# A four-layer graph network on one core: the engines' order from a planner with due times, or written out step by step

## The chip, the core and the metric

The kernel runs on one core of a Trainium2 chip. A core has five engines that run their own instruction lists and wait for each other through semaphores: TensorE (PE, matrix products into the banks of PSUM), VectorE (DVE), ScalarE (ACT), GpSimd (POOL) and SyncE (SP). Transfers are issued by SP or by POOL and carried by 16 transfer engines. The metric is the time of one execution on the device, in microseconds (us); lower is better.

## The reference

The input x holds 32 graphs of 512 nodes with 256 features, in float32, and one 512 x 512 adjacency matrix serves all graphs. Four layers follow each other; each ends with `x = layernorm(x + layer(x))`.

- Layer 0: attention with 8 heads of 32 features and the adjacency as mask, then a layernorm, a two-step perceptron (256 to 256, relu, 256 to 256) and another layernorm.
- Layer 1: graph attention with one head. The score of a pair of nodes is `leaky_relu(s1[n] + s2[m])`, masked, softmax, times the projected features.
- Layer 2: attention with full scores `h1 h2^T`, leaky relu, mask, softmax, times `h3`, relu.
- Layer 3: as layer 1 with 4 heads of 64 features, and elu at the end.

Node numbers matter nowhere but in the adjacency: if x, the adjacency's rows and columns and the output are all numbered in another order, the same thing is computed.

## The kernel before, in words

A graph's 512 nodes lie in 4 chunks of 128 partitions. The kernel does not loop over graphs at run time: Python writes out all steps of all 32 graphs and sorts them.

**Steps.** `fast_path` describes each graph as some 300 steps. A step names its engine, an assumed duration, what it reads and what it writes (`Plan.__call__`, through the helpers `dve`, `act`, `pool`). The work areas are slots of a few kinds: 8 PSUM banks, 8 "p" buffers (128 x 2048 numbers, for unnormalised attention weights), 9 "t", 7 "y", 6 "x" and so on.

**Layer 0** (`layer0`): x is transposed on PE (`transposed`, L932), q, k and v are projected (`project_t`, `project`, all through `product`, L749). For each half of the heads and each chunk m, `exps` makes the scores of four heads with four 32-row products side by side (L1064), ACT takes their exponential into p (L1068), DVE multiplies p by the adjacency (L1116), and four 32-column products side by side give the weighted sum (L1123). The row sums of the softmax are not taken on PE for each p: POOL issues transfers that add one p to another (`add_dma`, L1002), and only the total goes through PE (`sums`, L1095). In the last graph the sums are taken on PE at once. Then come `heads_out` (L1047), the normalisation (`normalise`) and the perceptron.

**Layers 1 and 3** turn a score into a product of exponentials. `gates` takes an exponential, transposes it on PE (L1212), writes it to DRAM through SP (L1216) and reads it back broadcast to all partitions (L1222). DVE then makes p (L1241 or L1320) and multiplies it by the adjacency (L1244 or L1327), and PE takes the product with the values (L749 in layer 1, L1335 in layer 3). **Layer 2** makes scores on PE, four steps on ACT and DVE, and a product with the values (L749).

**Shapes of TensorE.** Three shapes occur: the full array (128*128, way 0), four row tiles (32*128, way 1, `exps`) and four column tiles (128*32, way 2, L1123, L1335 and the sums). The products of `product` can run in way 0 or in way 2. `Plan.emit` chooses among them along the finished order.

**Order.** Up to six graphs are under way at a time. `Plan.place` simulates the engines with the assumed durations. At each point it takes, among the steps that can start first, the one that is due first. The due time of a step comes from `PACE` (81.87 us per graph), `TENTHS`, `FIRST` and `LAST`, tables that stretch a graph's own course. `START` holds back the first graphs. `safe` refuses a step that could leave too few buffers. The result is one fixed list per engine, and that is what runs on the chip.

**Set-up.** `prepare` loads weights and adjacency through SP, turns the adjacency into a transposed mask with 16 PE transposes (L818), and folds some weights together. These steps go ahead of all others on their engines.

Of the kernel before, what the change touches and what calls it, by code (L numbers as in the profile page):

```python
# [17 lines left out]
P = 128  # L18
# [11 lines left out]
WAYS = 6  # L30
PACE = 81.87
STAY = 0.00
START = (0, 10.17, 59.24, 97.18, 85.64)
EARLY = 186.52

TENTHS = (0, 35.72, 65.32, 68.92, 152.58, 202.32, 246.27, 266.73, 356.34, 362.66, 490.49)
FIRST = (
    (0, 35.72, 65.32, 62.35, 138.44, 202.98, 246.27, 266.73, 356.34, 362.66, 490.49),
    (-28.44, 35.72, 73.98, 55.02, 197, 202.32, 246.27, 266.73, 356.34, 362.66, 490.49),
    (-31.13, 30.72, 65.32, 68.92, 152.58, 202.32, 246.27, 266.73, 356.34, 362.66, 490.49),  # L40
    (0, 35.77, 65.37, 68.97, 152.63, 202.32, 246.27, 266.73, 356.34, 362.66, 490.49),)
LAST = (
    (0, 35.72, 65.32, 68.92, 152.58, 202.32, 246.27, 266.73, 354.73, 363.36, 490.49),
    (0, 35.72, 65.32, 68.92, 152.58, 202.32, 246.27, 266.73, 356.34, 362.66, 490.49),
    (0, 35.72, 65.32, 68.92, 152.58, 202.26, 246.21, 266.73, 356.34, 412.91, 557.81),
    (-0.21, 35.51, 65.11, 68.71, 152.37, 202.11, 226.96, 232.14, 316.44, 341.17, 500.04),
    (-6.23, 29.49, 59.09, 8.93, 61.49, 76.67, 155.18, 191.54, 257.43, 316.36, 394.47),)
# [391 lines left out]
SIGNAL = 70  # L439
SWITCH = 100  # L440
CHANGE = {0: 196, 1: 213, 2: 126}


class Slot:
# [3 lines left out]
    def __init__(self, kind):  # L448
        self.kind, self.index, self.users, self.ends, self.graph = kind, None if kind else 0, 0, 0.0, None
        self.first = self.last = None  # L450


class Op:
    def __init__(self, engine, ns, run, graph, rank, port, lag, tiling, ways):
        self.engine, self.ns, self.run, self.graph, self.rank = engine, ns, run, graph, rank
        self.port, self.lag, self.tiling, self.ways = port, lag, tiling, ways
        self.then, self.missing, self.slots, self.ready = [], 0, [], 0.0


class Plan:  # L460
# [10 lines left out]
    def clear(self):  # L471
        self.ops, self.graph, self.rank, self.start = [], 0, 0, 0.0
        self.log = {}

    def begin(self, graph, start=0.0):


        self.graph, self.rank, self.start = graph, 0, start

    def __call__(self, engine, ns, run, reads=(), writes=(), port=False, lag=0, tiling=0, ways=None):  # L480
        op = Op(engine, ns, run, self.graph, self.rank, port, lag, tiling, ways or {tiling: 0})
        if not op.rank:
            op.ready = self.start
        self.rank += 1
        needs = {}
        for is_write, group in ((False, reads), (True, writes)):
            for item in group:
                slot, part = (item[0], item[1:]) if isinstance(item, tuple) else (item, None)
                if slot not in op.slots:
                    op.slots.append(slot)  # L490
                    slot.users += 1
                    if slot.first is None:
                        slot.first = op.rank
                    slot.last = op.rank
# [19 lines left out]
    def profile(self, graph):  # L514

        ops = [op for op in self.ops if op.graph == graph]
        live = {kind: [0] * len(ops) for kind in self.counts}
        for slot in {id(s): s for op in ops for s in op.slots if s.kind}.values():
            for r in range(slot.first, slot.last + 1):
                live[slot.kind][r] += 1  # L520
        return live

    def place(self, urgency, ways, stay=0.0, early=1e12,):
# [3 lines left out]
        held_by = {g: self.profile(g) for g in {op.graph for op in self.ops}}  # L527
        engines = {e: 0.0 for e in (PE, DVE, ACT, POOL, SP, DMA)}
        waiting = {e: [] for e in engines}
        free = {k: [(0.0, i) for i in range(n)] for k, n in self.counts.items()}  # L530
        todo, held = {}, {}
        for op in self.ops:
            todo.setdefault(op.graph, set()).add(op.rank)
            if not op.missing:
                waiting[op.engine].append(op)
        order, front, ended = sorted(todo), {g: 0 for g in todo}, {}
        port, port_by, end, tiling = 0.0, None, 0.0, 0
        self.trace = []

        def safe(op, kind, new):  # L540
            spare = len(free[kind]) - len(new)
            if spare < 0:
                return False
            have = spare
            for g in order:
                mine = held.get((g, kind), [])
                have += len(mine)
                if g == op.graph:
                    have += len(new)
                    mine = mine + new  # L550
                r, rows = front[g], held_by[g][kind]
                ahead = sorted(s.first for s in mine if s.first > r)
                for i, stop in enumerate(ahead + [len(rows)]):
                    if stop > r and max(rows[r:stop]) + len(ahead) - i > have:
                        return False
                    r = max(r, stop)
                if g == op.graph:
                    return True

        while todo:  # L560
            choice = None
            for e, ops in waiting.items():
                found = []
                for op in ops:
                    if order[0] + ways <= op.graph:
                        continue
                    due = urgency(op)
                    t = max(engines[e], op.ready, ended.get(op.graph - ways, 0.0))
                    if op.graph >= 0:
                        t = max(t, due - early)  # L570
                    if op.port and port_by is not e:
                        t = max(t, port)
                    if choice and t > choice[0]:
                        continue
                    wants = {}
                    for s in op.slots:
                        if s.index is None:
                            wants.setdefault(s.kind, []).append(s)
                    if all(safe(op, kind, new) for kind, new in wants.items()):
                        for kind, new in wants.items():  # L580
                            t = max(t, sorted(free[kind])[len(new) - 1][0])
                        if op.tiling != tiling and e is PE:
                            due += stay
                        found.append((t, due, op))
                if found:
                    best = min(found, key=lambda f: f[:2])
                    if choice is None or best[0] < choice[0]:
                        choice = best
            assert choice, "no instruction can be placed: too few buffers"
            t, _, op = choice  # L590
            if op.engine is PE and op.tiling != tiling:
                t, tiling = max(t, engines[PE] + SWITCH), op.tiling
# [35 lines left out]
    def emit(self, tiling):  # L628
# [16 lines left out]
        for _, op in self.trace:  # L645
            if op.engine is PE:
                tiling[0] = chosen.pop()
            if op.run:
                op.run()
# [817 lines left out]
```

## Time and profile before

| | |
|---|---|
| median of 3 runs | 2868.73 us (2868.06 to 2869.86) |
| the profiled execution | 2871.61 us |
| its span, first to last instruction | 2869.7 us |
| TensorE busy | 2802.0 us (98%) |
| VectorE busy | 2436.6 us (85%) |
| ScalarE busy | 1884.6 us (66%) |
| GpSimd busy | 871.5 us (30%) |
| granted TensorE clock, mean | 0.991 |

The busy time of TensorE counts each matmul from its start to its modelled end, and matmuls overlap. A busy TensorE is therefore not one at its peak: the distance between the starts of two steps tells more than the length of one. Durations below come from the one profiled execution.

### The profile page before, as it was taken

How to read it: one execution, taken by the hardware profiler on the slowest of the kernel's cores; microseconds unless marked ns; L12 is line 12 of the kernel's file. 1: busy time of each engine (PE TensorE's matmuls, PEld its weight loads, DVE VectorE, ACT ScalarE, POOL GpSimd, SP SyncE). 2: the span in 40 equal slices, each digit the busy share in tenths (PEclk: the TensorE clock that was granted, in tenths of full speed). 3: DMA queues.
4: the chain of work that ended last, by engine and by line, in shares of the span. 5: the costliest groups of instructions: out<-in, count | busy, mean ns of one | idle time of the engine just before them, and what ended most of it. 6: DMA issues, size and time to landing. Idle time of an engine off the chain costs nothing.

```text
span 2869.7 us, 49717 instructions
## 1 busy us (share of the span) xinstructions
PE 2802.0 (98%) x19058; PEld 1507.2 (53%) x19058; DVE 2436.6 (85%) x4076; ACT 1884.6 (66%) x4104; POOL 871.5 (30%) x962
## 2 busy tenths in 40 slices
PE   8889999999999999999999999999999999999996
PEld 3345455555555555555555555555555555554562
DVE  5467888988888988888888888998888998889877
ACT  4566667666676666676666676666676766677553
POOL 1223333323333223333323333323333323333312
PEclk9899999999999999999999999999999999999998
DMA  7855777777776777777777777777777777775115
GB/s 168 169 115 122 159 159 151 156 156 149 164 162 151 155 157 149 162 166 149 155 156 149 162 165 154 149 156 148 163 165 157 148 159 149 160 165 114 41 51 139
DMA packets 101188, 425.07 MB, mean 148 GB/s; under 512 B 10256, under 2 KB 46224, under 8 KB 59152
## 3 DMA queue, kind: packets, MB, share of 16 engines
q0 software_dynamic: 49600, 325.08, 57.6%
q1 hardware_dynamic: 51344, 96.75, 11.7%
q8 instruction: 152, 2.49, 0.3%
q14 instruction: 92, 0.75, 0.1%
HBM read 63.38 MB, written 17.10 MB: 28 GB/s over the span
## 4 chain that ended last, share of the span: by engine, by line
PE 87%; DVE 7%; DMA 2%; ACT 2%; issue 2%; POOL 0%; SPq 0%; DVEq 0%; ACTq 0%; POOLq 0%
PE bank L749 54%; PE bank L1064 8%; PE bank L1123 8%; PE bank L1335 7%; PE bank L932 4%; DVE p L1116 3%; PE bank L1047 2%; PE bank L1311 1%; PE bank L1095 1%; PE bank L1015 1%; DVE p L1320 1%; DMA x<-in_x_dram 1%; ACT p L1068 1%; DVE st L973 1%; DMA p<-p 0%
## 5 line engine op out<-in xcount | busy, mean ns | idle before, releaser
L1002 POOL DMA_DIRECT2D p<-p x372 | 323.3, 873 | 1766.4 <-DMA p<-p 587.7
L1116 DVE TENSOR_TENSOR p<-p,edge_t 128x2048 f32<-128x2048 f32 x256 | 628.5, 2464 | 61.4 <-ACT p L1068 61.2
L920 ACT ACTIVATE t<-bank 128x512 f32<-128x512 f32 x640 | 373.1, 595 | 393.6 <-PE bank L1123 129.9
L1068 ACT ACTIVATE p<-bank 128x512 f32<-128x512 f32 x1024 | 537.4, 599 | 81.9 <-PE bank L1064 81.5
L749 PE MATMUL bank<-v,p 128*128 128x257 f32 (+1 forms) x2912 | 468.0, 384 | 4.3 <-DVE p L1244 3.8
L749 PEld LDWEIGHTS bank<-v,p 128*128 128x128 f32 (+1 forms) x2912 | 367.7, 159 | 90.7 <-issue 26.6
L973 DVE BATCH_NORM_STATS2 st<-y 128x6 f32<-128x256 f32 x768 | 316.1, 412 | 36.2 <-POOL y L990 26.6
L1320 DVE TENSOR_SCALAR p<-p,e,e 128x512 f32<-128x512 f32 x512 | 333.1, 684 | 0.4 <-DMA p<-row 0.3
L990 POOL TENSOR_TENSOR y<-y,x 128x512 f32<-128x512 f32 x192 | 275.3, 1441 | 156.7 <-ACT y L1295 98.4
L1327 DVE TENSOR_TENSOR p<-p,edge_t 128x2048 f32<-128x2048 f32 x128 | 310.2, 2423 | 2.2
L1064 PE MATMUL bank<-t,t 32*128 32x512 f32 x2048 | 300.7, 646 | 0.0
L983 ACT ACTIVATE x<-y,rs,rs 128x256 f32<-128x256 f32 x512 | 277.7, 596 | 18.0 <-DVE rs L980 15.1
L1123 PE MATMUL bank<-p,v 128*32 128x512 f32 x2048 | 274.0, 607 | 15.2 <-DVE p L1116 11.4
L1335 PE MATMUL bank<-p,v 128*32 128x512 f32 x2048 | 241.5, 597 | 3.7 <-DVE p L1327 3.2
L749 PE MATMUL bank<-t,wqkv 128*32 128x512 f32 (+1 forms) x944 | 243.8, 596 | 0.9 <-ACT t L920 0.9
L920 ACT ACTIVATE v<-bank 128x264 f32<-128x264 f32 (+2 forms) x384 | 176.1, 459 | 80.0 <-PE bank L749 77.0
L749 PE MATMUL bank<-t,t 128*128 128x512 f32 (+1 forms) x656 | 225.2, 592 | 0.0
L1064 PEld LDWEIGHTS bank<-t,t 32*128 32x128 f32 x2048 | 84.1, 185 | 173.4 <-issue 86.4
L932 PE MATMUL bank<-ident,x 128*128 128x128 f32 x1024 | 149.6, 280 | 14.2 <-DMA x<-in_x_dram 10.3
L974 DVE BATCH_NORM_AGGREGATE mv<-st 128x2 f32<-128x6 f32 x768 | 139.9, 182 | 26.3
L932 PEld LDWEIGHTS bank<-ident,x 128*128 128x128 f32 x1024 | 118.2, 142 | 78.8 <-issue 37.7
L749 PEld LDWEIGHTS bank<-t,t 128*128 128x128 f32 (+1 forms) x656 | 94.3, 167 | 111.2 <-issue 107.2
(119 smaller groups left out, 3855.7 us busy)
## 6 DMA issues: line engine op xcount, KB each, us to landing
p<-p POOLq DMA_DIRECT2D x248, 1024.0 KB, 7.2
p<-p POOLq DMA_DIRECT2D x124, 512.0 KB, 5.8
p<-row SPq DMA_DIRECT2D x32, 1024.0 KB
x<-in_x_dram SPq DMA_DIRECT2D x32, 512.0 KB
out_dram<-x SPq DMA_DIRECT2D x32, 512.0 KB
p<-p SPq DMA_DIRECT2D x31, 512.0 KB
e<-row SPq DMA_DIRECT2D x32, 256.0 KB
t<-in_adj_dram SPq DMA_DIRECT2D x4, 256.0 KB
```

Source lines behind the costliest of these rows:

```text
L749: nc.tensor.matmul(out[c:c + w, :], left[:, c:c + w], right, start=start, stop=stop)
L920: act(170 + n * 0.84, lambda: nc.scalar.activation(to(T(dst)), frm(T(src)), AF.Copy), [src], writes)
L932: nc.tensor.transpose(T(bank)[:, (2 * k + c) * P:(2 * k + c + 1) * P], T(src)[:, c0 + c, k * P:(k + 1) * P], ident)
L973: nc.vector.bn_stats(T(st)[:, c, :], T(y)[:, c, :])
L1002: nc.gpsimd.dma_start(a, b, accum_op=ALU.add)
L1064: nc.tensor.matmul(T(banks[j]), T(kT)[r, g, m * P:(m + 1) * P], T(qT)[r, g, :], start=True, stop=True)
L1068: act(600, lambda j=j: nc.scalar.activation(T(p)[:, j, :], T(banks[j]), AF.Exp, scale=1.0 / math.sqrt(D0)), [banks[j]], [(p, j)])
L1116: dve(2420, lambda p=p, m=m: nc.vector.tensor_tensor(T(p), T(p), T(edge_t)[:, m, :].unsqueeze(1).to_broadcast([P, J, N]), ALU.mult), [p, ( ...
L1123: nc.tensor.matmul(T(av)[j * D0:(j + 1) * D0, :], T(v)[:, m, h * D0:(h + 1) * D0], T(p)[:, j, :], start=(m == 0), stop=(m == NC - 1))
L1320: nc.vector.tensor_scalar(T(p)[:, 2 * m + i, :], T(G)[:, h, :], T(e1)[:, r:r + 1], T(e02)[:, r:r + 1], ALU.mult, ALU.max)
L1327: nc.vector.tensor_tensor(p4, p4, T(edge_t)[:, m0:m0 + 2, :].unsqueeze(2).to_broadcast([P, 2, 2, N]), ALU.mult)
L1335: nc.tensor.matmul(T(av)[w:w + 32, :], T(q)[:, m0 + m, 2 * H3 + k * P + w:2 * H3 + k * P + w + 32], T(p)[:, 2 * m + w // D3, :], start=(m0 ...
```

## The change

**The order is written out.** `place`, `safe`, the due times and their tables go away. In their place stands `ORDER`, a text for each engine. Each letter is a graph (a dot for the set-up, A to Z and a to f for the 32 graphs). A letter alone means "the next step of this graph on this engine"; a number n ahead of it means "the step that stands n places further on among those left". `Plan.follow` reads the texts, chooses the shape of each product along PE's text (`ways`) and hands out the buffers by a simulation with these fixed lists. The texts were found by a search whose step durations and transfer landings were varied at random.

**Durations and transfers in the model.** The assumed durations are replaced throughout (for instance 1717 for 1720 ns, 482 for 600 ns), and a tail is added per engine. All transfers of the graphs are modelled as one queue: `move` plans an issue on SP and a transfer, as `add_dma` does with an issue on POOL. The instructions that issue transfers stay on the engines where they were. These numbers steer the handing out of buffers; no instruction depends on them otherwise.

**Node numbers.** Chunk c of partition p holds node 4p + c, where it held node 128c + p. So a partition's four rows of x and of the output are one piece of 4 KB in DRAM. The adjacency is loaded and transposed to match, with a stride of four in the transposes.

The set-up steps have places in `ORDER` like all others; on SP's list the load of wqkv stands 16th, where it was first.

```diff
-WAYS = 6
-PACE = 81.87
-STAY = 0.00
-START = (0, 10.17, 59.24, 97.18, 85.64)
-EARLY = 186.52
...
+GRAPHS = ".ABCDEFGHIJKLMNOPQRSTUVWXYZabcdef"
+ORDER = {
+    "PE": (
+        "AA2.2...A2A1.2A.AA.1...A2.A1..1A1BB2AA2AA1BABAA1B1AB2ABA2ABABA1BCA2BC3BC4BB3C2C4BBBCCBCB1B2BBCDABABA"
...
+    "SP": (
+        "3.3.2.1.A11.11.9.9.4.12.9.2.7.1..6..4.B3.DC1.1..FEABAACBBAADCCBBEAGDDCCFBHEEDDGCIFFEEDHJGGFFIEKHHGGJ"
...
-SWITCH = 100
-CHANGE = {0: 196, 1: 213, 2: 126}
+SIGNAL = 40
+SWITCH = 92
+ENTRY = {1: 121, 2: 34}
+TAIL = {PE: 160, DVE: 85, ACT: 120, POOL: 130, SP: 0, DMA: 0}
...
+    def ways(self, order):
+        costs, steps = {0: 0.0, 1: 1e15, 2: 1e15}, []
+        for op in order:
+            came, new = {}, dict.fromkeys(costs, 1e15)
+            for way, extra in op.ways.items():
+                cost = {w: c + (SWITCH + op.enter(way) if w != way else 0) for w, c in costs.items()}
+                came[way] = min(cost, key=cost.get)
+                new[way] = cost[came[way]] + extra
+            costs = new
+            steps.append(came)
...
+    def follow(self, order):
+        left, queues = {}, {}
+        for op in self.ops:
+            left.setdefault((op.engine, op.graph), []).append(op)
+        for e, steps in order.items():
+            queues[e], at = [], 0
+            for step in steps:
+                if step.isdigit():
+                    at = 10 * at + int(step)
+                else:
+                    queues[e].append(left[e, GRAPHS.index(step) - 1].pop(at))
+                    at = 0
+        self.ways(queues[PE])
...
-                 adj[c * P:(c + 1) * P, :], 6000 + 700 * c)
+                 adj.rearrange("(p c) n -> p c n", p=P)[:, c, :], 6000 + 700 * c)
...
-                                        T(edges)[:, c, m * P:(m + 1) * P], ident)
-            plan(PE, 440, run, [edges], [bank])
+                                        T(edges)[:, c, m::NC], ident)
+            plan(PE, 854, run, [edges], [bank], entry=56)
...
+    def move(run, reads, writes, ns, lag):
+        started = Slot(None)
+        plan(SP, 350, run, reads, writes + [started])
+        plan(DMA, ns, None, reads + [started], writes, lag=lag)
...
-        plan(SP, 450, lambda xs=xs: nc.sync.dma_start(
-            T(xs), x[b].rearrange("(c p) d -> p c d", p=P)), [], [(xs, c) for c in range(NC)],
-            lag=9000)
+        move(lambda xs=xs: nc.sync.dma_start(T(xs), x[b].rearrange("(p c) d -> p c d", p=P)),
+             [], [(xs, c) for c in range(NC)], 1600, 2500)
...
-        plan.place(urgency, WAYS, 1e3 * STAY, 1e3 * EARLY)
+        plan.follow(ORDER)
         plan.emit(tiling)
```

## The prediction

> **What bounds the kernel now.** I read the page's totals first, then the waits of TensorE, then busy time in stretches of 100 us, then TensorE's instructions in order of time. The totals:
>
> ```profile
> PE 2802.0 (98%) x19058; PEld 1507.2 (53%) x19058; DVE 2436.6 (85%) x4076; ACT 1884.6 (66%) x4104; POOL 871.5 (30%) x962
> q0 software_dynamic: 49600, 325.08, 57.6%
> q1 hardware_dynamic: 51344, 96.75, 11.7%
> ```
>
> TensorE (PE) is the bound; VectorE (DVE) has 15% to spare, and the transfer engines are busy 69% of the time. The waits of PE, all of them longer than 2 us in total:
>
> ```profile
> PE bank L1123 <- DVE p L1116: 11.4, 13, 2.7
> PE bank L932 <- DMA x<-in_x_dram: 10.3, 2, 7.7
> PE bank L749 <- DVE p L1244: 3.8, 1, 3.8
> PE bank L1311 <- DVE p L1327: 3.6, 2, 2.7
> PE bank L1335 <- DVE p L1327: 3.2, 2, 2.2
> ```
>
> They are few and short (total, times, longest), so hardly any fall in the middle. By stretches (PE busy, PEld, DVE, ACT, POOL, granted clock, transfers):
>
> ```profile
> 0.00:100.00 100.00, 83.43 (x612) 34.71 (x612) 53.11 (x85) 51.56 (x99) 12.16 (x27) 0.93 0.80 176
> 100.00:200.00 100.00, 86.50 (x642) 41.01 (x635) 55.52 (x107) 54.40 (x115) 33.01 (x32) 0.90 0.66 132
> 1000.00:1100.00 100.00, 99.86 (x675) 53.54 (x668) 88.25 (x138) 66.75 (x149) 31.76 (x37) 1.00 0.75 162
> 2800.00:2870.00 70.00, 44.60 (x302) 17.84 (x301) 51.28 (x101) 26.67 (x59) 19.45 (x17) 0.88 0.59 137
> ```
>
> The loss is at the two ends: 30 us of idle PE and a lowered clock in the first 200 us, 25 us in the last 70. In between PE is never idle, so what is left there is how the busy time is spent. The timeline of PE in one such stretch (start, us, line, operands, tile shape, records):
>
> ```profile
> 576.92 1.90 PE L749 MATMUL bank<-v,p 128*128 128x257 f32 x8
> 578.75 1.14 PE L1064 MATMUL bank<-t,t 32*128 32x512 f32 x8
> 579.82 1.07 PE L1123 MATMUL bank<-p,v 128*32 128x512 f32 x8
> 580.82 1.09 PE L1047 MATMUL bank<-ident,t 128*128 128x128 f32 x8
> 581.75 0.60 PE L932 MATMUL bank<-ident,y 128*128 128x128 f32 x4
> 582.19 3.63 PE L749 MATMUL bank<-v,p 128*128 128x257 f32 x16
> 588.56 1.92 PE L749 MATMUL bank<-v,p 128*32 128x257 f32 x32
> 590.29 1.04 PE L1123 MATMUL bank<-p,v 128*32 128x512 f32 x8
> 591.15 1.90 PE L749 MATMUL bank<-t,w_sb 128*32 128x512 f32 x16
> ```
>
> Read starts, not lengths. The L1123 step takes 591.15 - 590.29 = 0.86 us between neighbours of the same tile shape (128*32), but 580.82 - 579.82 = 1.00 us where the shape changes after it. The L1064 step (32*128) takes 1.07 us. Its work is two passes of 512 columns, and a pass takes 0.429 us wherever the shape stays (start to start, all records), so 0.21 us of the 1.07 is change of shape.
>
> So I sorted every matmul record of the trace: each gets the time its own form takes beside an equal shape (0.109 us for 128 columns transposed, 0.216 for 256, 0.429 for 512), and what is over goes to a change of shape, to a lowered clock, or to idling. That gives 7.7 us before the first matmul, 2628.5 of work, 140.0 for 837 changes of shape (0.167 each), 55.0 idle, 19.5 at the lowered clock, 1.4 of crumbs, and 17.5 from the last matmul's start (2852.2) to the end: 2869.6, the span. Idle and lowered clock lie like this: 43.4 us before 200, 13.0 from 200 to 2700, 18.1 after. A graph (one of the 32 batch elements) takes (2504.60 - 520.35) / 23 = 86.3 us, from the starts of a repeating piece in the chain of work, with 26 changes of shape.
>
> **What the Trainium skill says.** "TensorEngine Tiling (Array Packing)", section Key Properties: "Mode switching requires drain". The trace agrees: 0.09 to 0.11 us before the first pass of the new shape, and for two of the shapes another 0.05 to 0.10 before the second. "TensorE: Matmul & The Clock Gate", Part 1: an idle window of about 3.4 us halves the clock. The trace agrees: besides the very start, the clock is halved six times between 58 and 181 us, for 3.4 or 6.8 us at a time, each after waits. "Trainium Kernel Development and Optimization", Key Constraints: transfers of all queues run on the same 16 engines. The two queue lines above show both on those engines.
>
> **The change part by part.** *No instruction is added or removed.* Both kernels hand each engine a fixed list; only how the list is found differs. "All transfers in one queue" describes the model of the search: the adds into p (L1002) are still issued by POOL and the rest by SP. The new durations in the code change no instruction. So three things can move time.
>
> *Changes of shape.* I read the new PE list off the diff, step by step against the list of PE steps in a graph, and chose the shape of the free steps (L749's products run either as 128*128 or 128*32) by the rule that the diff writes out. It has 714 changes, not 837. At the mean price this is 123 x 0.167 = 20.6 us. By kind it is less, since mostly the cheap entry into 128*32 went (326 to 249; into 32*128 254 to 244; into 128*128 257 to 221): with 0.13, 0.21 and 0.16 us for the three it is 9.7 + 2.1 + 5.8 = 17.6, and some more products run as 128*32 (271, not about 255, at 0.026 us more each, +0.4). I take -17 us. Bounds: -21, and -12 if the cheap kind costs only the 0.09 us seen at most entries.
>
> *Node = 4 x partition + chunk.* x and out move in runs of 4 KB, not 1 KB. In the transfer records a 1 KB packet takes 46 ns and an 8 KB one 309, so about 30 ns per 4 KB are saved, some 0.3 us of 16 engines per graph. Transfers of x are waited for twice (10.3 us above, of which 7.7 is the very first load), and the work on the engines keeps its shapes. The cover is PE's backlog; uncovered it is worth tenths of a us at either end. The 16 transposes of adj (L818) now read with a stride of four elements. They took 3.5 us at the halved clock (9.46 to 12.98). The trace has no strided read; between 0 and another 3.5, I take +2.
>
> *The order: the start.* Of the 43.4 us, 11.4 is L1123 waiting for the mask product, 2.6 the fourth graph's x and 3.8 L1244; the lowered clock (16.0) follows from such waits. The old list has places with nothing between a score step and its L1123: 53 to 72 us and 91 to 103, where PE runs exps and av of one graph alone. A score needs 4 exps (4 x 0.6 us) and one mask product (2.46), 4.9 us, before its L1123. In the new list the PE work between the two, summed with the durations above, is for the first three graphs 4.3 us at the least, 4.8 in the lowest tenth, 8.2 at the median. So nearly every such wait is covered. DVE is no bound: set-up takes it to about 30 us, as now (41 of its 47 set-up steps are still ahead of the first graph's), and 16 mask products add 39 us, while PE's own work up to the second graph's last L1123 ends near 90 us. Against it: SP's list puts the weights wqkv 16th instead of 1st. The 16th issue comes at 11.1 us now, and with 4 MB queued up to it and some 0.38 MB a us at best, it lands at about 15 us. The transposes of x and adj fill PE to about 14 to 16 us anyway, so I book 1 to 3 us within the lowered-clock time that is there already. About 5 us of slow start up to 33 us stays, some 8 of idle and 8 of lowered clock after it: 21 for 43. I take -22. Bounds: 0, and -37 if all after 33 us goes.
>
> *The order: the middle.* Three long chains decide, and I compared the cover that the lists give. Last score of a graph to its row sums (L1095), which needs 4.9 us and then four transfers, 7.2 + 7.2 + 5.8 (median landings) and about 4: 29 us. Old list 42.5 us, new 36.4 to 45.6 in the middle. Gate transpose (L1212) to L749 in layer 1: the shortest parts seen add up to 10.3 us, and the broadcast's landing varies by 2.2. Old 15.4, new 13.0 at least, 14.8 at the median. Last layer-2 score to its product: old 3.4, new 3.4. Each is covered, two of them by less than now. I take 0 for the 13.0 us. DVE rises from 88 to 89%.
>
> *The order: the end.* The last three layer-3 blocks need 3 x (16 x 0.68 + 4 x 2.42) = 62 us of DVE behind some 80 us of PE work, and the new list leaves 8.7 us between the last gate transpose and its first L1335, where 10 to 12 are needed. So some waiting stays. The normalisation and store after the last matmul stay 17 us. I take -4, bounds +8 and -10.
>
> Sum: -17 + 2 - 22 + 0 - 4 = -41 us against the profiled span of 2869.7, so 2828.7. The medians of the runs shown (2868.73) lie 1.0 under this span, which gives 2828 us. I work against the span because the profiled execution's own 2871.61 us holds 1.9 us outside it.
>
> **Rivals.** *Only the shapes* (0.19): the start is bounded by the dependence of the first graphs, whose loads open at nearly the same amount of PE work (third graph at 45.6 us of work now, 44.2 in the new list, fourth 71.8 and 67.5). Then 2869.7 - 17 + 2 - 1 = 2854. For it speaks that equal opening; against it that the waits sit at L1123 and not at x.
> *Nearly all idling goes* (0.15): idle and lowered clock fall from 74.5 to about 30 (5 at the first load, 12 at the end, 13 in the middle): 2809.
> *Slower by stalls in the middle* (0.11): a fixed list can't go round a late landing. If the row sums (L1095) wait for the adds, everything behind them on PE waits, and so do ScalarE and DVE. The price is the lateness times some 26 graphs; 41 / 26 = 1.6 us per graph cancels the gain. The lowest new cover, 36.4 us, would need the chain to take 38 instead of 29. At 3 us of lateness it ends at 2828 + 78 = 2906. Against it: the same line waited 1.3 us in all, once.
> *No difference* (0.05): 0.5 to 1.5 us per graph of such waits.
>
> **How the numbers follow.** The forecast's case (0.50) covers 2815 to 2842, with 2828 in the middle. The shape-only case covers 2842 to 2863, the best case 2795 to 2815. 2804 to 2864 holds the first two and over half of the third, 0.79. Within 0.2% (5.7 us, about what a measurement here can tell from no change) is 0.05, slower 0.11, faster 0.84.
>
> **What would show it.** About 714 changes of shape in PE's order and 22 per graph, at a period of about 85.5 us. L1123's wait for the mask product under 4 us. In the first 200 us PE busy above 90% and a clock above 0.95. The row sums, layer-1 and layer-2 products waiting no more than now in the middle. I am wrong if PE shows idle time in every stretch from 300 to 2600, or if the first 100 us look as now.

## The result, and the profile after

The changed kernel takes 2854.66 us (median; 2852.66 to 2857.78), the kernel before took 2869.86 us beside it (2868.06 to 2874.71). One more of the changed kernel's five runs took 4110.25 us at a granted clock of 0.653 and is left out. The ratio is 0.9946, with a 95% interval from 0.993 to 0.9961: 15 us faster, where the forecast was 41. The time lies where the rival "only the shapes" put it (2854), though not for that rival's reason. The span of the profiled execution went from 2869.7 to 2852.9 us.

The totals of the page, as shown of the kernel before:

```profile
PE 2780.6 (97%) x19322; PEld 1516.4 (53%) x19322; DVE 2314.9 (81%) x4076; ACT 1858.9 (65%) x4104; POOL 939.4 (33%) x962
...
q0 software_dynamic: 49600, 325.08, 58.2%
q1 hardware_dynamic: 26768, 96.75, 11.2%
```

TensorE still is the bound, with the same work to do. The packets of SP's queue are halved by the longer runs of x and out, and its share of the transfer engines fell from 11.7 to 11.2%. VectorE has 122 us less, GpSimd (POOL) 68 us more busy time with the same number of instructions: a step that is held up, as in the example below, counts as busy for as long as it is held.

By stretches (PE busy, PEld, DVE, ACT, POOL, granted clock, transfers):

```profile
0.00:100.00 100.00, 82.84 (x596) 35.71 (x596) 48.53 (x84) 48.87 (x97) 11.01 (x25) 0.93 0.76 181
100.00:200.00 100.00, 95.05 (x721) 48.10 (x721) 70.87 (x119) 66.78 (x142) 32.15 (x33) 0.98 0.68 136
1000.00:1100.00 100.00, 97.25 (x666) 52.52 (x662) 84.18 (x137) 66.20 (x147) 36.24 (x35) 1.00 0.72 153
2600.00:2700.00 100.00, 92.97 (x619) 50.17 (x612) 85.25 (x160) 62.12 (x140) 35.54 (x30) 0.97 0.24 55
```

The second 100 us gained, the first did not. The stretch at 1000 us was 99.86 busy and is 97.25 now: idle time has come into the middle. It is the lowest of the 24 stretches from 200 to 2600 us; ten of them show 100.00, so the idle time comes in lumps. From 2600 to 2700 us TensorE was busy for 98.56 us before and is for 92.97 now.

The waits of TensorE (total, times, longest), all over:

```profile
...
PE bank L1784 <- DMA x<-in_x_dram: 8.6, 1, 8.6
...
PE bank L2180 <- DVE p L2172: 6.3, 6, 2.1
...
PE bank L1974 <- DVE p L1967: 5.5, 8, 1.8
PE bank L1595 <- DMA wqkv<-in_L_gnn_w_qkv_dram: 5.0, 1, 5.0
```

L1974 is the old L1123 (first layer's weighted sum), L2180 the old L1335 (third layer's), L1595 the old L749 (`product`), L1784 the transposes. (The longest wait of the view, 9.1 us, is that of a small product at the very end, behind all graphs, and is not shown.) The wait for the first layer's mask product is halved, 11.4 to 5.5 us; a new one stands for the weights wqkv.

To see where the time went I sorted the matmul records of both traces again: *work* at the pace that a form keeps beside its own shape, *changes of shape* at a price for each pair of shapes (leaving the full array 0.095 us, 32*128 0.109, 128*32 0.114; entering 32*128 0.104, 128*32 0.025, the full array 0.055 for a transpose and 0.104 otherwise), and the *rest*, which here holds idling, the lowered clock and small gaps together, so that these numbers are not the prediction's own. Work is 2617.9 us in both. "The last matmul" is the last one of the graphs.

| part of the trace | before | after | difference |
|---|---|---|---|
| up to the first matmul | 7.7 | 8.6 | +0.9 |
| changes of shape (837, then 714) | 141.1 | 122.2 | -18.9 |
| rest, up to 33 us | 5.0 | 10.4 | +5.4 |
| rest, 33 to 200 us | 40.8 | 20.5 | -20.3 |
| rest, 200 to 2600 us | 14.6 | 26.6 | +12.0 |
| rest, 2600 us to the last matmul | 25.1 | 27.5 | +2.4 |
| last matmul to the end | 17.5 | 19.1 | +1.6 |
| sum of the differences | | | -16.9 |

So the shapes paid as forecast and the stretch from 33 to 200 us nearly so, and the middle, the first 33 us and the end took 22 us of it back. Each column is one execution: of two executions of nearly the same kernel, the changed one and the order alone (below), the whole rest is 85.0 and 82.7 us, so 2 or 3 us in a line of this table are not to be read. In the middle the waits of TensorE were these before (200 to 2600 us, 3.1 us in all),

```profile
PE bank L1123 <- DVE p L1116: 2.1, 8, 0.6
PE bank L749 <- ACT p L1068: 0.5, 1, 0.5
```

and are these after (14.5 us in all):

```profile
PE bank L1974 <- DVE p L1967: 4.6, 7, 1.8
PE bank L2180 <- DVE p L2172: 3.4, 4, 1.5
PE bank L2180 <- DVE rs L1832: 2.5, 1, 2.5
PE bank L1595 <- ACT t L1772: 1.6, 1, 1.6
```

Most name VectorE. One of them, followed back. VectorE in order of time (start, duration, line):

```profile
2032.52 2.28 DVE L1967 TENSOR_TENSOR p<-p,edge_t 128x2048 f32<-128x2048 f32 x1
2034.72 6.22 DVE L2165 TENSOR_SCALAR p<-p,e,e 128x512 f32<-128x512 f32 x3
...
2045.82 0.15 DVE L1832 SCALAR_TENSOR_TENSOR rs<-mv,rs 128x4 f32<-128x4 f32 x1
```

GpSimd at the same time:

```profile
2032.52 3.42 POOL L1842 TENSOR_TENSOR y<-y,bb_row 128x512 f32<-128x512 f32 x1
2035.89 1.76 POOL L1854 DMA_DIRECT2D p<-p  x2
2037.04 1.93 POOL L1842 TENSOR_TENSOR y<-y,x 128x512 f32<-128x512 f32 x1
2038.28 1.91 POOL L1842 TENSOR_TENSOR y<-y,g_row 128x512 f32<-128x512 f32 x1
```

And TensorE, in its brackets what it waited for:

```profile
2046.05 2.75 PE L2180 MATMUL bank<-p,v 128*32 128x512 f32 x16 [2.55 <-DVE rs L1832]
```

Three L2165 steps, which take 1.6 us at the median of their kind, took 6.22 while three tensor steps and two issues of GpSimd followed each other closely. GpSimd's own first step took 3.42 us, where the quickest of its kind takes 1.26 and the median 1.56, while VectorE's mask product (2.28 us) ran beside it. The 4.6 us passed down VectorE's list, which can't be reordered, to the normalisation (L1832) and through it to TensorE. In the Trainium skill, "SBUF — State Buffer", section "SBUF: two separate sides", says that these two engines share a pair of ports as "an exclusive lock, not a bandwidth split": whichever starts first has it for its whole instruction. The 6.22 and the 3.42 us fit that; the trace does not show the ports themselves.

The hold as such is not new, though. It fell with the change, as the third layer's steps show, before and after (busy us, mean ns):

```profile
L1320 DVE TENSOR_SCALAR p<-p,e,e 128x512 f32<-128x512 f32 x512 | 333.1, 684 | 0.4 <-DMA p<-row 0.3
L2165 DVE TENSOR_SCALAR p<-p,e,e 128x512 f32<-128x512 f32 x512 | 290.1, 597 | 5.8 <-DMA p<-row 4.4
```

What grew is VectorE's waiting for what GpSimd hands it, shown with the experiments.

### The profile page after: what moved, and what is told of

The parts are those of the page before. It is cut to its first block, busy times and chain, and to the rows that moved or that the text cites. A ratio compares the mean times of both kernels' runs of the same rounds, so it can differ in the third digit from the quotient of the medians.

```text
span 2852.9 us, 50322 instructions
## 1 busy us (share of the span) xinstructions
PE 2780.6 (97%) x19322; PEld 1516.4 (53%) x19322; DVE 2314.9 (81%) x4076; ACT 1858.9 (65%) x4104; POOL 939.4 (33%) x962
## 3 DMA queue, kind: packets, MB, share of 16 engines
q0 software_dynamic: 49600, 325.08, 58.2%
q1 hardware_dynamic: 26768, 96.75, 11.2%
## 4 chain that ended last, share of the span: by engine, by line
PE 84%; DVE 8%; DMA 3%; ACT 3%; issue 2%; POOL 0%; SPq 0%; ACTq 0%; DVEq 0%; POOLq 0%
PE bank L1595 53%; PE bank L1916 8%; PE bank L2180 7%; PE bank L1974 6%; PE bank L1784 5%; DVE p L1967 3%; PE bank L1899 2%; DMA p<-p 1%; DVE p L2165 1%; PE bank L2156 1%; PE bank L1947 1%; PE bank L1867 1%; DMA p<-row 1%; ACT p L1920 1%; DVE st L1825 1%
## 5 line engine op out<-in xcount | busy, mean ns | idle before, releaser
L1967 DVE TENSOR_TENSOR p<-p,edge_t 128x2048 f32<-128x2048 f32 x256 | 618.3, 2420 | 89.3 <-ACT p L1920 88.8
L1920 ACT ACTIVATE p<-bank 128x512 f32<-128x512 f32 x1024 | 563.9, 599 | 150.7 <-PE bank L1916 129.6
L1595 PE MATMUL bank<-v,p 128*128 128x257 f32 (+1 forms) x2792 | 468.4, 381 | 3.1 <-DVE p L2089 3.1
L1595 PEld LDWEIGHTS bank<-v,p 128*128 128x128 f32 (+1 forms) x2792 | 368.0, 161 | 94.4 <-issue 25.8
L1842 POOL TENSOR_TENSOR y<-y,x 128x512 f32<-128x512 f32 x192 | 289.2, 1513 | 347.9 <-ACT y L2140 209.7
L2165 DVE TENSOR_SCALAR p<-p,e,e 128x512 f32<-128x512 f32 x512 | 290.1, 597 | 5.8 <-DMA p<-row 4.4
L2172 DVE TENSOR_TENSOR p<-p,edge_t 128x2048 f32<-128x2048 f32 x128 | 294.0, 2299 | 1.0
L1974 PE MATMUL bank<-p,v 128*32 128x512 f32 x2048 | 263.8, 598 | 5.6 <-DVE p L1967 5.5
L2180 PE MATMUL bank<-p,v 128*32 128x512 f32 x2048 | 248.1, 597 | 8.9 <-DVE p L2172 6.3
L1595 PE MATMUL bank<-t,wqkv 128*32 128x512 f32 (+1 forms) x1088 | 247.1, 609 | 7.7 <-DMA wqkv<-in_L_gnn_w_qkv_dram 5.0
L1595 PE MATMUL bank<-t,t 128*128 128x512 f32 (+1 forms) x656 | 228.1, 593 | 1.6 <-ACT t L1772 1.6
L1772 ACT ACTIVATE v<-bank 128x512 f32<-128x512 f32 (+2 forms) x384 | 169.4, 456 | 90.5 <-PE bank L1595 89.7
L1784 PE MATMUL bank<-ident,x 128*128 128x128 f32 x1024 | 146.3, 280 | 15.3 <-DMA x<-in_x_dram 8.6
L1784 PEld LDWEIGHTS bank<-ident,x 128*128 128x128 f32 x1024 | 116.9, 142 | 82.4 <-issue 27.7
L1835 ACT ACTIVATE y<-y,rs,rs 128x256 f32<-128x256 f32 x256 | 143.5, 596 | 17.0 <-DVE rs L1832 16.6
```

What stands on the lines that cost most here:

```text
L1595: nc.tensor.matmul(out[c:c + w, :], left[:, c:c + w], right, start=start, stop=stop)
L1772: act(55 + n * 0.83, lambda: nc.scalar.activation(to(T(dst)), frm(T(src)), AF.Copy), [src], writes)
L1784: nc.tensor.transpose(T(bank)[:, (2 * k + c) * P:(2 * k + c + 1) * P], T(src)[:, c0 + c, k * P:(k + 1) * P], ident)
L1835: act(492, lambda c=c: nc.scalar.activation(T(dst)[:, c, :], T(y)[:, c, :], AF.Identity, bias=T(nm)[:, c:c + 1], scale=T(rs)[:, c:c + 1]), ...
L1920: act(482, lambda j=j: nc.scalar.activation(T(p)[:, j, :], T(banks[j]), AF.Exp, scale=1.0 / math.sqrt(D0)), [banks[j]], [(p, j)])
L1967: dve(2205, lambda p=p, m=m: nc.vector.tensor_tensor(T(p), T(p), T(edge_t)[:, m, :].unsqueeze(1).to_broadcast([P, J, N]), ALU.mult), [p, ( ...
```

## The experiments

Theory: (1) the shapes gained what the count says; (2) the late wqkv costs the start 5 to 7 us; (3) the middle lost because the new lists let GpSimd's steps come between VectorE and TensorE, the more so as TensorE itself got faster. The rivals to it: the numbering costs something; the transfers that add come too late; VectorE's or ScalarE's own load is what TensorE runs into.

### The two halves of the change apart

The order with the old numbering, and the numbering with the old order. Of the changed kernel, for the first (x and out likewise):

```diff
-                 adj.rearrange("(p c) n -> p c n", p=P)[:, c, :], 6000 + 700 * c)
+                 adj[c * P:(c + 1) * P, :], 6000 + 700 * c)
-                                        T(edges)[:, c, m::NC], ident)
+                                        T(edges)[:, c, m * P:(m + 1) * P], ident)
```

> The written-out order alone, with the rows of a graph numbered as in the kernel before. Theory (all of the change lies in the order, the numbering of the nodes costs and gives nothing): 2853 to 2857 us, as the changed kernel. Rival (the strided reads of the numbering cost time, my term of +2 us): 2851 to 2853 us.

> The new numbering alone, with the order of the kernel before. Theory: no difference from the kernel before, within 1.5 us of it, because the 16 strided transposes showed the same pace as plain ones and the adjacency loads were hidden. Rival (the numbering costs or gives something): more than 3 us away, either way.

Measured: the order alone 2853.62 us (2852.34 to 2858.61), ratio to the kernel before 0.9948 (0.9933 to 0.9964). The numbering alone 2869.04 us beside 2871.41 for the kernel before, ratio 0.9994 (0.9985 to 1.0002). All of the gain is in the order; whether the numbering gives a us or two can't be told from these.

### The shapes

```diff
-    tiling, either = [0], {0: 0, 2: 26}
+    tiling, either = [0], {0: 0}
```

> The changed kernel's order, but every product that may choose its shape takes the whole array, so that the shape changes by count are 945 in place of 714. Theory (a change of shape holds up TensorE by what its kind showed in the trace, 160.0 us in all against 125.8): 34 us over the changed kernel, so about 2889 us. Rival (the changes are mostly hidden behind waits, or the 32 wide pieces of the products cost more than the trace's matmul records show, so that taking them away gives that back): under 15 us over it, about 2855 to 2869 us.

Measured: 2883.46 us, 29.8 over the order alone on the same chip. By the prices of the accounting the 945 changes of its trace cost 164.8 us where 714 cost 122.2, and the rest fell from 82.7 us (order alone) to 67.3. So a change costs 0.18 us on TensorE, but only 0.13 us net (29.8 / 231). The theory's 34 us came within 4 us of the time, but with less for the changes than the accounting's 42.6 us and nothing for what comes back: a slower TensorE waits less for the others. Its waits in the middle fell from 13.5 us (order alone) to 7.9:

```profile
PE bank L1974 <- DVE p L1967: 2.5, 5, 1.7
PE bank L2180 <- DVE p L2172: 2.2, 2, 1.3
PE bank L2180 <- DVE rs L1832: 1.1, 1, 1.1
```

### The first weights

SP's list with the load of wqkv behind the first graph's x; the other numbers count places among those left, so they fall by one.

```diff
-        "3.3.2.1.A11.11.9.9.4.12.9.2.7.1..6..4.B3.DC1.1..FEABAACBBAADCCBBEAGDDCCFBHEEDDGCIFFEEDHJGGFFIEKHHGGJ"
+        "3.3.2.1.A.10.10.8.8.3.11.8.1.6..6..4.B3.DC1.1..FEABAACBBAADCCBBEAGDDCCFBHEEDDGCIFFEEDHJGGFFIEKHHGGJF"
```

> The changed kernel with one step moved in the transfer queue: the first weight load, 16th there, goes out right behind the first graph's input. Theory (the late landing at 18.3 us idles TensorE for 5 us and its clock falls to half after that): 5 to 7 us under the changed kernel, so 2848 to 2850 us against 2854.7. Rival (the 15 loads behind it come later instead, and the mask or the attention that waits for them moves the wait on): within 2 us of the changed kernel.

Measured: 2848.63 us, 6.0 under the changed kernel's median and 5.0 under the order alone on its own chip; ratio to the kernel before 0.9932 (0.9918 to 0.9945). It has the lowest median of the kernels here that do the whole computation, but its runs reach from 2847.52 to 2855.11 us, and its interval overlaps that of the order alone, so the size of the gain is rough. The start of the changed kernel, TensorE in order of time:

```profile
18.37 5.92 PE L1595 MATMUL bank<-t,wqkv 128*128 128x512 f32 x8 [4.96 <-DMA wqkv<-in_L_gnn_w_qkv_dram]
...
40.09 1.06 PE L1974 MATMUL bank<-p,v 128*32 128x512 f32 x8
```

And with the earlier load:

```profile
13.48 3.60 PE L1595 MATMUL bank<-t,wqkv 128*128 128x512 f32 x8
18.79 0.58 PE L1684 MATMUL bank<-be_col,y 128*128 128x1 f32 x4 [1.71 <-DMA y<-in_L_gnn_w_dram]
...
36.49 1.06 PE L1974 MATMUL bank<-p,v 128*32 128x512 f32 x8
```

The wait of 4.96 us is gone, one of 1.71 us appears behind it, and the first weighted sum starts 3.6 us sooner, which is what the trace shows of the 5 to 6.

### A shorter TensorE in both orders

One of the four products of the first layer's hidden matrix is left out in every graph, 27.5 us of TensorE's work in all; the same edit in both kernels:

```diff
-                for k in range(KC):
+                for k in range(KC if d else 1):
                     product(T(bank), T(w1_sb)[:, k, d * P:(d + 1) * P], T(nT)[:, k, :],
-                                     start=(k == 0), stop=(k == KC - 1))
+                                     start=(k == 0), stop=(k == (KC if d else 1) - 1))
```

> The kernel before with TensorE's work made 27.5 us shorter and everything else, its order too, left: of the four products of the first layer's hidden matrix in every graph one is left out (32 products of 0.8585 us; half of the hidden values then lack a term). Theory (a faster TensorE catches up with the engines behind it, and waits give part of the gain back, also in the order of the kernel before): 15 to 20 us under the kernel before, with the idle rest between 200 and 2600 us up from 15 to 22 to 27 us. Rival (the old order has no such waits, the stalls belong to the new list alone): 26 to 27.5 us under it, the rest unchanged at 15 us.

> The changed kernel with the same product left out of every graph, 27.5 us of TensorE's work. Theory (waits give back part, more of it the faster TensorE already is): 10 to 18 us under the changed kernel, the idle rest between 200 and 2600 us up from 27 to 36 to 42 us. Rival (the stalls have causes of their own and do not depend on TensorE's pace): 26 to 27.5 us under it, the rest at 27 us.

Measured: 2856.23 us beside 2871.81, so 15.6 of the 27.5 us arrive in the old order; 2843.43 us, so 11.2 arrive in the new one (from the changed kernel's 2854.66). Both fall within the theory's ranges, with their rest in the middle (22.9 and 41.5 us) too. The waits of the middle: 3.1 to 9.6 us in the old order, nearly all of it the mask product,

```profile
PE bank L1123 <- DVE p L1116: 8.3, 18, 1.3
PE bank L1335 <- DVE p L1327: 0.9, 3, 0.5
```

and 14.5 to 19.2 us in the new one, whose rest rose by more (26.6 to 41.5), in part because its clock was halved three times in the middle for 3.4 us each, once without the edit. Neither order has much room behind TensorE: of what TensorE saves about half is lost again, in the old list too.

### What TensorE runs into

GpSimd's steps short: 320 of its 384 tensor steps work on 8 of their 256 columns, so the residuals and biases of the other columns are left out (of the changed kernel; the same edit to the kernel before; the y buffers start at zero in both):

```diff
         w = slice(c0, c0 + 2)
+        n = 8 if row is not g1_row else C
         pool(1235, lambda: nc.gpsimd.tensor_tensor(
-            T(dst)[:, w, :], T(a)[:, w, :],
-            T(b)[:, w, :] if row is None else T(row).unsqueeze(1).to_broadcast([P, 2, C]), op),
+            T(dst)[:, w, :n], T(a)[:, w, :n],
+            T(b)[:, w, :n] if row is None else T(row)[:, :n].unsqueeze(1).to_broadcast([P, 2, n]), op),
```

> The changed kernel with 320 of GpSimd's 384 tensor steps on 8 of their 256 columns (the residuals and biases of the other columns are left out), so that GpSimd has about 350 us less to do and blocks VectorE less. Theory A (the waits of the middle come from GpSimd's steps, which hold VectorE up and hand it its input late): the idle rest between 200 and 2600 us falls from 27 to 15 us or less, and the time to 2840 to 2844 us. Theory B (they come from the transfers that add, or from VectorE and ScalarE alone): within 3 us of the changed kernel, the rest above 23 us.

> The kernel before with the same 320 of GpSimd's 384 tensor steps on 8 of 256 columns. Theory A (in the old order GpSimd's steps cost TensorE little, so that the loss in the middle is the new list's exposure to them): 6 to 12 us under the kernel before, the idle rest between 200 and 2600 us from 15 to 6 to 10 us. Rival (GpSimd costs both orders the same, so that it can't be why the new one gained less): 20 to 27 us under it.

Measured: the changed kernel with short steps 2829.96 us, ratio to the kernel before 0.9856 (0.9839 to 0.9872), 24.7 us under the changed kernel and more than either theory asked for. The kernel before with short steps 2857.82 us, ratio 0.9961 (0.9947 to 0.9975), 10.8 under its own. That time fits theory A, but the rest of the middle fell to 0.8 us, below the 6 to 10 expected: GpSimd was behind nearly all of the 14.6 us that the old middle lost, more than theory A gave it. TensorE's waits in the middle, changed kernel with short steps (2.3 us in all, 14.5 without):

```profile
PE bank L1978 <- DVE p L1971: 0.8, 1, 0.8
PE bank L1598 <- ACT t L1775: 0.7, 1, 0.7
```

With most of GpSimd's work out of the way the change is worth 27.9 us (2857.82 to 2829.96) where it is worth 15.2 with it. So GpSimd accounts for some 13 us of the 26 that the forecast was off (the two short kernels ran on different chips; by their ratios it is 15).

It does not account for most of the loss in the middle, though. By the accounting of the traces the short steps took the rest of the middle from 26.6 to about 8 us in the changed kernel and from 14.6 to 0.8 in the kernel before. So GpSimd costs the middle of both orders, some 18 and 14 us, and only 4 or 5 of the 12 us that the middle lost by the change are its own (give or take the 2 or 3 us named above). Another 5 or so of the 13 lie between 33 and 200 us. What makes up the other 7 or so is not shown; the runs with a faster and a slower TensorE speak for less room behind TensorE as one part.

GpSimd acts in two ways, which these runs do not separate: VectorE is held, and it gets its input late. How much VectorE is held is not what the change made worse, though where it falls may be: summed over VectorE's steps, the time above the quickest tenth of their kind was 257 us before and is 174 after (53 and 70 with short steps). GpSimd's own steps show 97 us of such excess before and 202 after, which fits a GpSimd that is held longer itself and hands over later. VectorE's waits in the middle for GpSimd's sums, before:

```profile
DVE st L973 <- POOL y L990: 24.3, 29, 1.6
```

After:

```profile
DVE st L1825 <- POOL y L1842: 69.3, 60, 3.9
```

With short steps:

```profile
DVE st L1828 <- POOL y L1846: 15.3, 26, 2.8
```

Half of the first layer's mask products left out:

```diff
-                    T(p), T(p), T(edge_t)[:, m, :].unsqueeze(1).to_broadcast([P, J, N]), ALU.mult),
+                    T(p)[:, :, :256], T(p)[:, :, :256],
+                    T(edge_t)[:, m, :256].unsqueeze(1).to_broadcast([P, J, 256]), ALU.mult),
```

> The changed kernel with the first layer's 256 mask products of VectorE on half of their columns (the other half of the scores stays unmasked), about 1.1 us less each, 280 us less for VectorE. Theory A (GpSimd's steps and their lock make the waits): the waits fall partly, 3 to 8 us under the changed kernel. Theory C (VectorE's own load is what TensorE runs into, wherever its queue is long): the idle rest between 200 and 2600 us falls from 27 to under 15 us, and the time to 2838 to 2845 us. Rival (ScalarE or the transfers): within 2 us of it.

Measured: 2843.18 us, 11.5 under the changed kernel; the rest of the middle fell from 26.6 to 14.1 us, the waits from 14.5 to 6.4. It lies past theory A's 8 us and inside theory C's ranges: VectorE's queue is what TensorE runs into. But 261 us off VectorE (2314.9 busy to 2053.8) gave less than 330 us off GpSimd (939.4 to 609.3), although no wait of TensorE names GpSimd. I read the two theories as two ends of one chain, GpSimd late for VectorE and VectorE late for TensorE; the example above shows one such case, and how many of the waits are of that kind was not counted.

The adding transfers cut short (372 of them):

```diff
-            nc.gpsimd.dma_start(a, b, accum_op=ALU.add)
+            nc.gpsimd.dma_start(a[:, 0:1, :128], b[:, 0:1, :128], accum_op=ALU.add)
```

To keep the numbers finite, the ones that pick the sums became fours, and the mask's zeros 0.01.

> The changed kernel with the 372 transfers that add one half of the exponentials to the other cut to 128 values of one row each (the row sums are then wrong, since the rest isn't added; the issues on GpSimd's queue and all else stay). Theory A (GpSimd's tensor steps make the waits of the middle): within 4 us of the changed kernel, the idle rest between 200 and 2600 us above 22 us. Theory B (buffers that the adding transfers give free late hold up ScalarE's exponentials): the rest falls from 27 to 15 us or less and the time to 2840 to 2846 us.

Measured: 11834.55 us, which tells nothing, since these sums leave the range that the fast part of the kernel accepts and its general part ran after it. The fast part can be read by itself, up to 2830 us: its waits in the middle are 15.9 us (14.5 in the changed kernel) and the rest 36.2 (26.6), for a reason that was not followed. The small product behind all graphs starts at 2846.45 us, at 2843.14 in the changed kernel. Nothing was gained by quick transfers, which speaks against theory B; as only one trace of an abnormal run shows it, it is support and no more.

### Two versions meant to be faster

The earlier wqkv, and GpSimd's 64 steps for the second norm's bias as transfers that add; in the second version also the first half of the feed-forward bias.

```diff
-            add(xs, xs, None, c0, be2_row)
+            add_row(xs, be2_row, c0, 2)
...
+    def add_row(dst, row, c0, n):
+        w, parts = slice(c0, c0 + n), [(dst, c) for c in range(c0, c0 + n)]
+        def run():
+            nc.gpsimd.dma_start(T(dst)[:, w, :], T(row).unsqueeze(1).to_broadcast([P, n, C]),
+                                accum_op=ALU.add)
+        started = Slot(None)
+        plan(POOL, 850, run, [row] + parts, parts + [started], lag=300)
+        plan(DMA, 625 * n, None, [row, started] + parts, parts, lag=1900)
```

> A version meant to beat both: the changed kernel with the first weight load right behind the first graph's input (6 us under the changed kernel in its own run), and GpSimd's 64 steps that add the second norm's bias to the residual issued as transfers that add, 64 of 256 KB; the residual is needed tens of us later. If GpSimd's steps make the waits (320 short steps gave 24.7 us): those 64 give about a fifth, 3 to 5 us, on top, so 2843 to 2846 us. Rival (an issue of 0.87 us on GpSimd costs as much as the step of 1.56 us, or the 16 MB more on its queue make the row sums' transfers late): 2848 us or above.

> As the run beside it, and of the two steps that add the feed-forward bias in a graph the first, which had 6 to 23 us to spare in the trace, as a transfer too. If GpSimd's steps make the waits: another 1 to 3 us, so 2841 to 2845 us. Rival (the later landing takes up the spare time, and the sum behind it waits in VectorE's queue): at or above the run beside it.

Measured: 2870.11 us (2861.42 to 2875.91) and 2873.29 us (2855.99 to 2880.25), as slow as the kernel before (ratios 0.9998 and 1.0005). Both lie in the rivals' ranges. GpSimd's group in the changed kernel (busy, mean ns):

```profile
L1842 POOL TENSOR_TENSOR x<-x,be_row 128x512 f32<-128x512 f32 x64 | 101.5, 1608 | 0.2
```

And with the transfers:

```profile
L1853 POOL DMA_DIRECT2D x<-be_row x64 | 93.4, 1528 | 0.9 <-POOL y L1842 0.9
```

An issue with a row repeated as its source took 1528 ns, not the 902 of the other adds, so GpSimd saved 8 us of 101. The queue's packets rose from 49600 to 67008, which is 272 for each such 256 KB, and its share of the transfer engines from 58.2 to 61.8%. TensorE's waits in the middle rose to 33.3 us, 8.8 of it one wait for a layer-1 mask product:

```profile
PE bank L1595 <- DVE p L2100: 9.4, 3, 8.8
```

That wait leads back to a transfer of SP's queue, the broadcast of a layer-1 gate: issued at 1059.06 us, it landed 9.1 us later, and VectorE waited 5.95 us for it. VectorE's waits for these broadcasts in the middle were 1.2 us in the earlier-wqkv version, and with the added transfers they are

```profile
DVE p L2097 <- DMA e<-row: 15.6, 6, 5.9
```

So the broadcasts kept VectorE waiting longer beside the added transfers. That these were the cause of all 21 us over the earlier-wqkv version is not shown.

## Why the prediction was right or wrong, step by step

- **Shapes, -17: right.** 714 changes as counted, 141.1 to 122.2 us, -18.9. What the step left out is that the gain is not paid in full: 0.13 us net a change against 0.18 on TensorE.
- **Strided transposes, +2: nothing.** At the halved clock a strided one took 0.213 us, as a plain one did; the last four of the 16 already ran at the full clock, in 0.11 to 0.12 us. The numbering alone shows no difference in time.
- **Transfers of x and out, tenths of a us: right.** The saving itself was put at 0.3 us a graph; from the packet times named beside it nearly 0.5 follows, and the fall of the queue's share (11.7 to 11.2%) gives about as much.
- **The start, -22: right in its mechanism, 7 or 8 us short.** From 33 to 200 us the rest fell by 20.3. The mask product's wait fell from 11.4 to 5.5 us all over (I had said under 4): in the first 200 us from 9.3 to 0.9, while in the middle it rose from 2.1 to 4.6. I had put all 11.4 into the start, where only 9.3 of it lay. The sign named for being wrong, a first 100 us that looks as before, did come: TensorE was busy for 83.43 us and is for 82.84. What failed is "I book 1 to 3 us within the lowered-clock time that is there already" for the load of wqkv: it landed at 18.3 us and not at 15, TensorE idled 4.96 us, and the rest up to 33 us grew by 5.4. Moving that load gave some 5 us.
- **The middle, 0: wrong, and this is the step that failed.** It was +12.0. I compared the cover of three long chains on TensorE's list, with median durations, and found each covered. They were: the row sums waited 0.2 us in all (L2156), and the stalls of that rival did not come. Most of the stalls sit at short links that I took as given, the mask products and normalisations on VectorE. Two terms are missing. A list packed more tightly on TensorE has less room behind it: 27.5 us off TensorE brought 15.6 in the old order. And VectorE's list is exposed to GpSimd: its waits for GpSimd's sums in the middle went from 24.3 to 69.3 us. Of the 12 us the short steps give 4 or 5 to GpSimd; what the other 7 or so come from stays open, with the lack of room as the likeliest part. VectorE's share was forecast to rise to 89% there, and in the stretch at 1000 us it fell to 84.18: its load did not grow, its inputs came later. The waits listed as all those over 2 us left out three of TensorE for ScalarE (3.0, 2.3 and 2.1 us). The sign that I read past was in the page of the kernel before: its chain that ended last already ran through VectorE for 7%.

The chain of the kernel before, by engine:

```profile
PE 87%; DVE 7%; DMA 2%; ACT 2%; issue 2%; POOL 0%; SPq 0%; DVEq 0%; ACTq 0%; POOLq 0%
```

Of the changed kernel:

```profile
PE 84%; DVE 8%; DMA 3%; ACT 3%; issue 2%; POOL 0%; SPq 0%; ACTq 0%; DVEq 0%; POOLq 0%
```

And of the changed kernel with GpSimd's steps short:

```profile
PE 93%; DMA 3%; ACT 2%; DVE 2%; issue 0%; SPq 0%; ACTq 0%; POOL 0%; POOLq 0%; DVEq 0%
```

A busy share of 98% hid it: GpSimd is on none of these chains by name, and yet with its steps short VectorE falls from 8 to 2%, and in the kernel before from 7 to 2%.
- **The end, -4: wrong by 8.** After 2600 us the rest rose by 2.4 us, and 1.6 came after the last matmul; the rise is near what two traces differ by, but the gain did not come. Short steps of GpSimd leave it as it is (26.6 against 27.5), and so do half mask products (27.7), so it is neither of these; which dependence of the last two graphs sets it was not tried.
- **The sum.** -41 became -17 against the span: 2 more from the shapes, 2 from the transposes that cost nothing, 7 or 8 less at the start with the first load, 12 less in the middle, 8 less at the end. The rival "only the shapes" met the number with a start that gains nothing and a quiet middle; the trace shows a start that gains 14 us and a middle and end that lose them.

## What to carry to other kernels

Where one engine is busy 98% of the time, a saving on it need not be paid out in full: ask how much room the engines behind it have, in their own fixed order, before booking it (here about half was lost again). Cover is to be checked on every engine's list, not on the bounding one's alone, and with the durations that a held engine shows, not with medians. An engine that no wait of the bounding one names can still be the root: here short steps of GpSimd, at 33% busy, were worth 24.7 us to the changed kernel and 10.8 to the kernel before. And a cost that both kernels have explains a difference between them only by as much as it grew: it takes the same experiment on both to see that.

## What the runs showed of the hardware that I had not expected

- Three VectorE steps of some 0.54 us took 6.22 us beside a close row of GpSimd steps, and a GpSimd step of 1.26 us at its quickest took 3.42 beside a VectorE product of 2.28. Shortening 320 of GpSimd's steps brought the mean of that step from 597 to 538 ns over the whole kernel.
- A transfer that adds a repeated row costs GpSimd 1528 ns to issue, an adding transfer from a plain source 902.
- Reading the adjacency with a stride of four float32 values in the transposes cost nothing at the halved clock (0.213 us for 128 columns, strided or plain). At the full clock the few there were took 0.11 to 0.12 us, plain ones 0.109.
